# Masking the scores of a sparse graph-attention layer in PSUM with a signed bound, in place of multiplying the exponentials by mask bytes

## The chip, the cores and the metric

The kernel runs on one core of one Trainium2 chip, in one launch. The metric is the device time of that launch in microseconds (us). The kernel before was timed three times: 2150.40, 2150.49 and 2156.22 us, median 2150.49. A profile was taken of one execution of it.

A core has five engines, each with its own instruction queue that it works off in order: PE (TensorE, matrix products), DVE (VectorE, elementwise work and reductions), ACT (ScalarE, functions of one input with a scale and a bias), POOL (GpSimd, here mostly the engine that issues gathers) and SP (SyncE, here a queue for DMAs). SBUF is the on-chip working memory of 128 partitions. PSUM holds the results of products[...].

## What is computed

Two graph layers over 4096 nodes with 512 features each. The adjacency `adj` is 4096 x 4096 float32, symmetric in where it is nonzero, with a full diagonal; an off-diagonal entry is nonzero with a chance of a bit under 0.8%. The change is in the second layer:

```python
# layer 0
h = relu(layernorm(x));  x = x + relu(normalized(adj) @ h @ W0 + b0)
# layer 1
h = relu(layernorm(x))
Wh = h @ W;  e = leaky_relu(Wh @ a[:F] + (Wh @ a[F:]).T, 0.2)
mask = adj > 0
attention = softmax(where(mask, e, -1e12), axis=1)
negative_attention = -softmax(where(mask, -e, -1e12), axis=1)
out = elu(concat([attention @ h, negative_attention @ h], axis=1) @ wtrans)
x = x + out
```

So for each node i layer 1 needs, over the neighbours j of i, the weights exp(e) and exp(-e) with e = leaky_relu(s_i + t_j), their sums, and the sums of h_j with these weights.

## The kernel before

**Layer 0** is dense. It reads `adj` and its transpose, normalizes, and multiplies. On the way it also prepares layer 1: it writes one row per node into a table in HBM (eight copies, one for each eighth of the nodes i). A row has 644 words: the 512 features of h, the score t in word 512 (`ROW_T`), and from word 516 (`ROW_W`) on 512 mask bytes, one for each node of that eighth, which are 1 where the two nodes are neighbours and 0 elsewhere. It also lists, for each pair of 64-node blocks, the rows that these blocks need.

**Layer 1** (`sparse_layer1`, L1316) works by blocks of 64 nodes i (`RB`). There are 64 blocks, two to a pair. The first pair (`PAIR0`) is worked within layer 0 by code of its own (L1203 to L1313); the other 31 pairs, 62 blocks, are the loop that the change touches. Per pair:

- `gather1` (L1340) issues 22 indirect DMAs from POOL through `gather` (L469, the issue itself is L473): each fetches 128 table rows into SBUF. The 22 chunks go into three tiles, a = 0, 1, 2, with 8, 6 and 8 chunks. The even block of the pair uses tiles 0 and 1, the odd block tiles 1 and 2. Six tile slots exist, so two pairs are held at a time, and a gather has to wait until the block that used its slot two pairs earlier has been worked through.
- `weights(r)` (L1351) makes the weights of a block r, in two parts, one for each of its two tiles: 8 chunks x 64 nodes (128 x 512 elements) and 6 chunks (128 x 384). For each part, `scores` (L486, DVE at L487) adds t and s into a PSUM bank `z`; ACT makes `y` = 0.2 z (L1361); DVE takes the larger of the two into z (L1362); `exps` (L491, ACT at L499) writes exp(z) and exp(-z) into the SBUF tile `p` for g = 0 and 1; `mask_out` (L503, DVE at L509) multiplies each of the two by (mask byte > 0), in place in `p`, the mask bytes being read from the gathered rows. After both parts DVE sums the whole of `p` over its chunks into `total` (L1367).
- `product(r)` (L1370) multiplies the weights with the gathered rows on PE, 44 instructions (L516), makes the inverse sums (L540 on PE, L542 and L543 on DVE), and ACT writes the scaled result `us` (L1383).
- `turn(r)` (L1385) transposes `us` on PE (`tp`, L550), and ACT copies it to `ut` (L555).
- `finish1(j)` (L1390), once per pair, multiplies by `wtrans` with 16 instructions on PE (L1397), takes elu and adds x (L1405 to L1409), and stores.

**The order.** The loop from L1438 on lists, for step k: `product` of block k, the gathers of the pair two ahead (tile 0 at an even step, tiles 1 and 2 at an odd one), `weights` of block k + 2, `turn` of block k - 1, and at odd steps `finish1`. That is the program's order. Where nothing is pinned with `keep_in_program_order`, a planner may place instructions of one engine in another order, as far as their data allow. In the trace it has done so: on DVE the scores of a block's second part often stand ahead of the mask products of its first part, and on ACT `us` of an even block k stands behind the exponentials of both parts of block k + 2. The gathers are pinned, and so are the exponentials of the first four blocks.

Of the kernel before, what the change touches and what calls it, by code (L numbers as in the profile page):

```python
# [8 lines left out]
F32 = mybir.dt.float32  # L9
U8 = mybir.dt.uint8  # L10
# [3 lines left out]
AF = mybir.ActivationFunctionType  # L14
ALU = mybir.AluOpType
# [4 lines left out]
P = 128  # L20
# [10 lines left out]
RB = 64  # L31
# [16 lines left out]
ROW_W = 516  # L48
ROW = 644
MAXS = 40.0  # L50
TINY = 2.0**-110


# [214 lines left out]
def gcn_gat_kernel(  # L268
# [26 lines left out]
    nc = tc.nc  # L295
# [15 lines left out]
    RPT = NR // NTAB  # L311
# [12 lines left out]
    def bank(name):  # L324
        return ps.tile([P, 512], F32, tag="ps", name=name)
# [4 lines left out]
    with sbuf(name="init", bufs=1) as init:  # L330
        column = init.tile([P, P], F32, name="column")
        nc.vector.memset(column[:, 0:1], 0.0)
        n = 1
# [150 lines left out]
    def scores(s, z, t):  # L484

        n = z.shape[1]  # L486
        return nc.vector.tensor_tensor(  # L487
            z, t.to_broadcast([P, n, RB]), s.unsqueeze(1).to_broadcast([P, n, RB]), ALU.add
        )

    def exps(z, p, bound=False, pin=False, leaky=True):  # L491

        if leaky:
            nc.vector.scalar_tensor_tensor(z, z, ALPHA, z, ALU.mult, ALU.max)
        if bound:
            nc.vector.tensor_scalar(z, z, 2 * MAXS, -2 * MAXS, ALU.min, ALU.max)
        z = z.rearrange("p k (h i) -> p k h i", h=2)
        for g in range(2):
            i = nc.scalar.activation(p[:, :, :, g], z, AF.Exp, scale=(1.0, -1.0)[g])  # L499
            if pin:  # L500
                tc.keep_in_program_order(i)

    def mask_out(r, p, mask):  # L503

        m = mask[:, :, r % RPT * RB : (r % RPT + 1) * RB]
        m = m.rearrange("p k (h i) -> p k h i", h=2)
        for g in range(2):
            e = p[:, :, :, g]
            nc.vector.scalar_tensor_tensor(e, m, 0.0, e, ALU.is_gt, ALU.mult)  # L509
# [50 lines left out]
    with sbuf(name="y0", bufs=1) as y_pool, sbuf(name="wa", bufs=1) as wa_pool, sbuf(name="bits", bufs=4) as bits_pool, sbuf(name="small0", bufs=4) as small, ExitStack() as rest, ExitStack() as lists:  # L560
# [224 lines left out]
        def scale(yp, j):  # L785

            rs = small.tile([P, 2], F32, tag="rs", name=f"rs{j}")
            nc.vector.tensor_reduce(rs[:, 0:1], parts.pop(j), AX.X, ALU.add)
            nc.vector.tensor_scalar(rs[:, 1:2], rs[:, 0:1], TINY, None, ALU.max)
            nc.vector.reciprocal(rs[:, 1:2], rs[:, 1:2])  # L790
# [209 lines left out]
        i0, n = GROUPS[0]  # L1000
# [89 lines left out]
        def judge(small):  # L1090
# [11 lines left out]
            for g, vec in enumerate((s_all, t_all)):  # L1102
# [3 lines left out]
                nc.vector.tensor_scalar(  # L1106
                    ok[:, 2 + g : 3 + g], ok[:, 2 + g : 3 + g], MAXS * MAXS, None, ALU.is_le
                )
# [94 lines left out]
        with sbuf(name="work2", bufs=2) as work, sbuf(name="sums2", bufs=2) as sum_pool, sbuf(name="at2", bufs=4) as at_pool, sbuf(name="scratch", bufs=1) as scratch, sbuf(name="pair", bufs=1) as pair:  # L1203
# [95 lines left out]
            k = late0 % EJ  # L1299
# [16 lines left out]
    def sparse_layer1():  # L1316
        nonlocal verdict
        with ExitStack() as pools:

            def pool(name, bufs):  # L1320
                return pools.enter_context(sbuf(name=name, bufs=bufs))
# [3 lines left out]
            g_pools = {s: pool("g%d%d" % s, 1) for s in slots}  # L1325
            tmp, small, p_pool = pool("tmp", 1), pool("small1", 2), pool("p", 3)
            work, ut_pool, s_pool, wt_pool = pool("work1", 2), pool("ut", 2), pool("s", 2), pool("wt", 1)
            warm = small.tile([P, 1], F32, tag="warm", name="warm", bufs=1)
            nc.scalar.activation(warm, sign, AF.Exp)
            wt_sb = wt_pool.tile([P, 2 * FC, F], F32, name="wt_sb")  # L1330
# [15 lines left out]
            def parts(r):  # L1346

                t = gath[r // 2][r % 2 : r % 2 + 2]
                return (t[0], 0, t[0].shape[1]), (t[1], t[0].shape[1], t[1].shape[1])

            def weights(r):  # L1351

                nk = sum(CHUNKS[r % 2 : r % 2 + 2])
                p = p_pool.tile([P, nk, 2, 2, SB], F32, tag="p", name=f"p{r}")
                s = srow[r // 8][:, r % 8 * RB : (r % 8 + 1) * RB]

                for gt, k, n in parts(r):
                    z = bank(f"z{r}_{k}")[:, : n * RB].rearrange("p (k c) -> p k c", c=RB)
                    scores(s, z, gt[:, :, ROW_T : ROW_T + 1].bitcast(F32))
                    y = tmp.tile([P, n, RB], F32, tag=f"y{n}", name=f"y{r}_{k}")  # L1360
                    nc.scalar.activation(y, z, AF.Copy, scale=ALPHA)  # L1361
                    nc.vector.tensor_tensor(z, z, y, ALU.max)  # L1362
                    exps(z, p[:, k : k + n], leaky=False, pin=r in first)
                    mask_out(r, p[:, k : k + n], gt[:, :, ROW_W:].bitcast(U8))
                total = small.tile([P, 2 * RB], F32, tag="total", name=f"total{r}", bufs=3)
                q = p.rearrange("p k h g i -> p (h g i) k")
                nc.vector.tensor_reduce(total, q, AX.X, ALU.add)  # L1367
                wgt[r] = (p, total)
# [46 lines left out]
            first = order[:4]  # L1415
# [14 lines left out]
            for a in range(3):  # L1430
                gather1(pairs[1], a)
            weights(order[0])
            weights(order[1])

            tc.keep_in_program_order(
                nc.scalar.dma_start(out=wt_sb, in_=wtrans.rearrange("(c p) f -> p c f", p=P))
            )
            for k, r in enumerate(order):  # L1438
                product(r)
                if k % 6 == 1 and k // 6 < len(later):  # L1440
                    for j, n in GROUPS[-2:]:
                        queue = nc.scalar if k == 1 else nc.sync
                        tc.keep_in_program_order(copy_rows(queue, later[k // 6], j, n))
                if k + 4 - k % 2 < len(order):
                    for a in ((0,), (1, 2))[k % 2]:
                        gather1(order[k + 4 - k % 2] // 2, a)
                if k + 2 < len(order):
                    weights(order[k + 2])
                    if wanted and order[k + 2] % 8 == 7:
                        load_s(wanted.pop(0))  # L1450
                if k:
                    turn(order[k - 1])
                if k == 2:
                    finish1(PAIR0)
                if k == 40:
                    verdict = judge(small)
                if k % 2 and k > 1:
                    finish1(order[k - 3] // 2)
            turn(order[-1])
            finish1(order[-1] // 2)  # L1460

    sparse_layer1()
    bad = nc.values_load(
        verdict[0:1, 0:1],
# [38 lines left out]
```

## Time and profile before

| | us |
|---|---|
| three timed runs: lowest, median, highest | 2150.40, 2150.49, 2156.22 |
| the profiled execution: span from its first to its last instruction | 2033.7 |
| the median less that span | 116.8 |
| first gather of the 31 pairs; the last one ends | 1086.2; 1981.8 |
| PE's last instruction ends | about 2024 |

For the profiled execution the span is the only time on record; what lies around it is read here from the median of the timed runs. Times in the profile are counted from the span's start. A row of a view by groups names line, engine, operation and tiles (output first), the shapes, how many there were (x...), their busy time, the mean in ns, and then the idle time of the engine just before them and who ended it. In a timeline a row gives start, length, engine, line and operation, and in brackets the idle time before it. The granted clock of PE is 0.976 of full on average over the span.

### The profile page before, as it was taken

How to read it: one execution, taken by the hardware profiler on the slowest of the kernel's cores; microseconds unless marked ns; L12 is line 12 of the kernel's file. 1: busy time of each engine (PE TensorE's matmuls, PEld its weight loads, DVE VectorE, ACT ScalarE, POOL GpSimd, SP SyncE). 2: the span in 40 equal slices, each digit the busy share in tenths (PEclk: the TensorE clock that was granted, in tenths of full speed). 3: DMA queues.
4: the chain of work that ended last, by engine and by line, in shares of the span. 5: the costliest groups of instructions: out<-in, count | busy, mean ns of one | idle time of the engine just before them, and what ended most of it. 6: DMA issues, size and time to landing. Idle time of an engine off the chain costs nothing.

```text
span 2033.7 us, 23721 instructions
## 1 busy us (share of the span) xinstructions
PE 1884.8 (93%) x7832; PEld 1066.1 (52%) x7832; DVE 1279.9 (63%) x2907; ACT 626.0 (31%) x1181; POOL 932.4 (46%) x1047
## 2 busy tenths in 40 slices
PE   6999999897999999979996799999999999999998
PEld 3433337786788888868771233333333333333333
DVE  6555558989793538983354566566665656566653
ACT  5766652212112221212032233233322332333321
POOL 3000001133331113233064777777777777777770
PEclk9999999998999999989997899999999999999999
DMA  9988869467448565728384989989898898888880
GB/s 364 328 298 283 298 201 325 135 217 244 137 142 280 187 232 173 250 87 287 93 258 142 324 291 307 290 288 307 275 308 282 292 310 274 279 265 271 278 274 30
DMA packets 181115, 503.53 MB, mean 248 GB/s; under 512 B 27091, under 2 KB 35699, under 8 KB 180982
## 3 DMA queue, kind: packets, MB, share of 16 engines
q0 software_dynamic: 73184, 275.36, 42.1%
q1 hardware_dynamic: 77808, 171.80, 25.6%
q10 hardware_dynamic: 29990, 54.75, 7.7%
q8 instruction: 64, 1.05, 0.2%
q14 instruction: 69, 0.57, 0.1%
HBM read 409.89 MB, written 103.02 MB: 252 GB/s over the span
## 4 chain that ended last, share of the span: by engine, by line
POOL 16%; PE 13%; DMA 9%; issue 7%; DVE 4%; ACT 1%; DVEq 0%; POOLq 0%
POOL g L473 16%; DMA g<-table,idx 9%; PE u L516 7%; PE o L1397 5%; DVE p L509 1%; DVE z L487 1%; PE tp L550 1%; ACT p L499 1%; DVE z L1362 1%; ACT us L1383 0%; DMA table<-h 0%; DVE prod L895 0%; DVE stb L455 0%; DVE total L1367 0%; ACT y L1361 0%
## 5 line engine op out<-in xcount | busy, mean ns | idle before, releaser
L473 POOL DMA_INDIRECT g<-table,idx x704 | 701.4, 996 | 230.0 <-issue 209.3
L516 PE MATMUL u<-g,p 128*64 128x512 f32 x2816 | 628.6, 602 | 18.0 <-DVE p L509 13.2
L516 PEld LDWEIGHTS u<-g,p 128*64 128x64 f32 x2816 | 199.4, 139 | 394.1 <-issue 354.4
L972 PE MATMUL p<-t,sums 128*128 128x256 f32 x896 | 268.5, 384 | 15.2 <-DVE sums L960 10.4
L972 PE MATMUL p<-y,at 128*128 128x256 f32 x896 | 272.0, 386 | 3.6 <-DVE w L855 2.5
L487 DVE TENSOR_TENSOR z<-g,s 128x512 f32<-128x512 f32 (+1 forms) x124 | 78.4, 634 | 311.2 <-DMA g<-table,idx 298.1
L972 PE MATMUL p<-y,sums 128*128 128x256 f32 x896 | 270.6, 384 | 0.8 <-DVE sums L962 0.8
L1361 ACT ACTIVATE y<-z 128x512 f32<-128x512 f32 (+1 forms) x124 | 67.5, 544 | 553.1 <-DVE z L487 427.0
L1397 PE MATMUL o<-wt_sb,ut 128*128 128x512 f32 x512 | 228.3, 599 | 0.5 <-ACT ut L555 0.5
L432 POOL DMA_INDIRECT ld<-li,off x112 | 102.8, 918 | 258.7 <-DMA ld<-li,off 199.2
L812 ACT ACTIVATE m<-at 128x1024 uint8<-128x1024 f32 x110 | 115.0, 1053 | 339.7 <-DMA at<-in_adj_t 289.5
L1367 DVE TENSOR_REDUCE total<-p 128x128 f32<-128x1792 f32 x62 | 201.5, 3250 | 2.1
L972 PEld LDWEIGHTS p<-t,sums 128*128 128x128 f32 x896 | 171.8, 193 | 41.9 <-DVE sums L960 12.8
L972 PEld LDWEIGHTS p<-y,at 128*128 128x128 f32 x896 | 171.3, 193 | 32.1 <-DVE w L855 3.7
L972 PEld LDWEIGHTS p<-y,sums 128*128 128x128 f32 x896 | 173.1, 193 | 25.6 <-DVE sums L962 1.2
L509 DVE SCALAR_TENSOR_TENSOR p<-g,p 128x384 f32<-128x384 uint8 (+1 forms) x256 | 145.5, 619 | 23.3 <-ACT p L499 23.3
L821 POOL DMA_DIRECT2D table<-m x71 | 56.4, 795 | 220.3 <-ACT m L812 136.2
L747 ACT ACTIVATE junk<-ar 128x1024 bf16<-128x1024 f32 x128 | 134.7, 1052 | 72.1 <-DMA ar<-in_adj 70.8
L1397 PEld LDWEIGHTS o<-wt_sb,ut 128*128 128x128 f32 x512 | 96.0, 193 | 109.8 <-issue 108.9
L972 PE MATMUL p<-t,at 128*128 128x256 f32 x448 | 136.8, 388 | 9.6 <-DVE w L855 7.6
L499 ACT ACTIVATE p<-z 128x512 f32<-128x512 f32 (+2 forms) x252 | 123.6, 549 | 65.2 <-DVE z L1362 56.5
L776 PE MATMUL yp<-w_sb,hx_t 128*128 128x512 f32 x256 | 120.1, 613 | 2.9 <-DVE hx_t L729 2.9
(198 smaller groups left out, 1811.7 us busy)
## 6 DMA issues: line engine op xcount, KB each, us to landing
ar<-in_adj SPq DMA_DIRECT2D x128, 512.0 KB, 7.5
at<-in_adj_t SPq DMA_DIRECT2D x112, 512.0 KB, 4.1
table<-h ACTq DMA_DIRECT2D x182, 258.0 KB, 5.9
table<-m POOLq DMA_DIRECT2D x55, 256.0 KB, 4.9
g<-table,idx POOLq DMA_INDIRECT x704, 4.5
at<-in_adj_t SPq DMA_DIRECT2D x32, 256.0 KB, 7.8
xr<-in_x SPq DMA_DIRECT2D x32, 256.0 KB, 6.5
x1d<-y POOLq DMA_DIRECT2D x32, 256.0 KB, 5.3
```

The source lines that it names most:

```text
L432: return nc.gpsimd.indirect_dma_start(out=lst_dram[g][:, :], out_offset=bass.IndirectOffsetOnAxis(ap=off[g][:, e, c : c + 1], axis=0), in_ ...
L473: i = nc.gpsimd.indirect_dma_start(out=gt[:, k, :], out_offset=None, in_=table[2 * n // RPT], in_offset=bass.IndirectOffsetOnAxis(ap=idx[n ...
L487: return nc.vector.tensor_tensor(z, t.to_broadcast([P, n, RB]), s.unsqueeze(1).to_broadcast([P, n, RB]), ALU.add)
L499: i = nc.scalar.activation(p[:, :, :, g], z, AF.Exp, scale=(1.0, -1.0)[g])
L509: nc.vector.scalar_tensor_tensor(e, m, 0.0, e, ALU.is_gt, ALU.mult)
L516: i = nc.tensor.matmul(u[h * RB : (h + 1) * RB], p[:, k, h].rearrange("p g i -> p (g i)"), row(k), start=k == HALVES[r % 2][h][0], stop=en ...
L747: nc.scalar.activation(junk, ar, AF.Identity, accum_out=part[:, c : c + 1]),
L776: nc.tensor.matmul(yp, hx_t[j][:, c * P : (c + 1) * P], w0_sb[:, c, :], start=c == 0, stop=c == FC - 1,)
L812: nc.scalar.activation(m, at, AF.Sign)
L972: i = nc.tensor.matmul(out, left[:, x * P : (x + 1) * P], right, start=jp == 0 and first, stop=jp == NP - 1 and (final or not first),)
L1367: nc.vector.tensor_reduce(total, q, AX.X, ALU.add)
L1397: nc.tensor.matmul(po, ut[:, g, c, :], wt_sb[:, g * FC + c, :], start=g == 0 and c == 0, stop=g == 1 and c == FC - 1,)
```

## The change

`weights` no longer calls `exps` and `mask_out`. ACT makes from the mask bytes a float32 tile `m` that holds +1000 where the byte is 1 and -1000 where it is 0. DVE makes y = max(-m, z), which is z at a neighbour and 1000 elsewhere, and z = min(z, m), which is z at a neighbour and -1000 elsewhere. The exponentials are then taken of z and of -y, so that both vanish elsewhere. The pair worked within layer 0 keeps `exps` and `mask_out`.

```diff
@@ constants
+FAR = 1000.0
@@ sparse_layer1
+            far = small.tile([P, 1], F32, tag="far", name="far", bufs=1)
+            nc.gpsimd.memset(far, -FAR)
@@ weights(r), for each of the two parts
                     scores(s, z, gt[:, :, ROW_T : ROW_T + 1].bitcast(F32))
+                    m = tmp.tile([P, n, RB], F32, tag=f"m{n}", name=f"m{r}_{k}")
+                    bits = gt[:, :, ROW_W:].bitcast(U8)
+                    nc.scalar.activation(
+                        m,
+                        bits[:, :, r % RPT * RB : (r % RPT + 1) * RB],
+                        AF.Identity,
+                        scale=2 * FAR,
+                        bias=far,
+                    )
                     y = tmp.tile([P, n, RB], F32, tag=f"y{n}", name=f"y{r}_{k}")
                     nc.scalar.activation(y, z, AF.Copy, scale=ALPHA)
                     nc.vector.tensor_tensor(z, z, y, ALU.max)
-                    exps(z, p[:, k : k + n], leaky=False, pin=r in first)
-                    mask_out(r, p[:, k : k + n], gt[:, :, ROW_W:].bitcast(U8))
+                    nc.vector.scalar_tensor_tensor(y, m, -1.0, z, ALU.mult, ALU.max)
+                    nc.vector.tensor_tensor(z, z, m, ALU.min)
+                    for g, x in enumerate((z, y)):
+                        i = nc.scalar.activation(
+                            p[:, k : k + n, :, g],
+                            x.rearrange("p k (h i) -> p k h i", h=2),
+                            AF.Exp,
+                            scale=(1.0, -1.0)[g],
+                        )
+                        if r in first:
+                            tc.keep_in_program_order(i)
```

## The prediction

> **What bounds the kernel now.** The change touches only the loop over the 31 pairs, so I read that stage alone, first by slices of 40 us (columns: length, busy us and instructions of each engine, PE clock, DMA share, GB/s).
>
> ```profile
> 1560.00:1600.00 40.00, 37.22 (x156) 13.95 (x153) 22.79 (x33) 11.03 (x23) 30.57 (x32) 0.96 0.92 311
> 1840.00:1880.00 40.00, 38.80 (x160) 15.10 (x160) 26.26 (x37) 12.83 (x28) 30.56 (x32) 1.00 0.87 268
> 1960.00:2000.00 40.00, 38.48 (x172) 14.62 (x170) 24.44 (x36) 11.96 (x27) 16.84 (x17) 1.00 0.56 183
> ```
>
> PE is busy 93 to 97%, DVE 60%, ACT 30%. POOL shows only 76%, but the same 31 or 32 gathers in every slice until they are all issued. The waits of this stage (1160 to 2034) say what that means:
>
> ```profile
> POOL g L473 <- issue: 179.0, 588, 0.3
> ...
> PE tp L550 <- ACT us L1383: 27.4, 21, 2.9
> ```
>
> POOL's idle time is 0.3 us ahead of each gather, never more: no slot, no semaphore holds it up, it is working flat out. PE loses 27.4 us, all at one place: the transpose of an even block waits for `us`, which stands in ACT's queue behind exponentials that wait for gathered rows. The chain of waits from 1100 on agrees:
>
> ```profile
> by line: POOL g L473 32.2%; DMA g<-table,idx 18.2%; issue 14.0%; PE u L516 13.4%; PE o L1397 11.4%; DVE p L509 2.3%; DVE z L487 1.6%; PE tp L550 1.4%; DVE z L1362 1.3%; ACT p L499 1.2%; ACT us L1383 0.7%; DVE total L1367 0.3%; ACT y L1361 0
> ```
>
> Now the two paces. PE without a wait needs 27.46 us per pair (in its timeline the products with `wtrans` start at 1610.31 and 1637.77 with no idle entry between). POOL starts a gather every 1302.6 ns on average (622 intervals from 1170 to 1982): 22 x 1.3026 = 28.66 us per pair. So POOL sets the pace and PE waits about 1.2 us per pair; 28 pairs of that are the 27 us above. But most gathers are faster. POOL's and DVE's timelines of the same stretch:
>
> ```profile
> 1516.41 0.95 POOL L473 DMA_INDIRECT g<-table,idx  x1 [0.30 <-issue]
> 1517.66 1.33 POOL L473 DMA_INDIRECT g<-table,idx  x1 [0.31 <-DMA g<-table,idx]
> 1519.29 0.95 POOL L473 DMA_INDIRECT g<-table,idx  x1 [0.30 <-DVE z L1362]
> 1520.54 1.11 POOL L473 DMA_INDIRECT g<-table,idx  x1 [0.30 <-issue]
> 1521.96 0.94 POOL L473 DMA_INDIRECT g<-table,idx  x1 [0.30 <-issue]
> ```
>
> ```profile
> 1517.48 1.29 DVE L509 SCALAR_TENSOR_TENSOR p<-g,p 128x512 f32<-128x512 uint8 x2
> 1518.69 0.56 DVE L1362 TENSOR_TENSOR z<-z,y 128x384 f32<-128x384 f32 x1
> 1519.80 1.03 DVE L509 SCALAR_TENSOR_TENSOR p<-g,p 128x384 f32<-128x384 uint8 x2 [0.56 <-ACT p L499]
> 1520.87 3.25 DVE L1367 TENSOR_REDUCE total<-p 128x128 f32<-128x1792 f32 x1
> ```
>
> The gathers at 1517.66 and 1520.54 start inside a mask product (L509) and last 1.33 and 1.11 us; those beside L1362 and the reduction keep 0.95. I set every gather of the stage beside the DVE instruction that runs at its start. Of 84 that start within L509, 79 are stretched; within the scores (L487), 18 of 47; within L1362 0 of 62, within L1367 0 of 151, beside an idle DVE 0 of 230. The stretch is what is left of the DVE instruction less 0.125 us. Over the layer all stretches sum to 34.8 us, 28.0 of them by L509 and about 6 by L487.
>
> [...]L509 reads mask bytes and `p`, both in SBUF, L487 reads t and s, both in SBUF; L1362 has one input in PSUM. [...]
>
> **The change part by part.**
>
> ```profile
> L509 DVE SCALAR_TENSOR_TENSOR p<-g,p 128x512 f32<-128x512 uint8 x118 | 75.9, 684 | 1.8 <-ACT p L499 1.8
> L509 DVE SCALAR_TENSOR_TENSOR p<-g,p 128x384 f32<-128x384 uint8 x116 | 59.5, 554 | 15.7 <-ACT p L499 15.7
> ...
> L1362 DVE TENSOR_TENSOR z<-z,y 128x512 f32<-128x512 f32 x58 | 40.0, 689 | 3.5
> L1362 DVE TENSOR_TENSOR z<-z,y 128x384 f32<-128x384 f32 x58 | 32.4, 558 | 0.0
> ...
> L1408 DVE SCALAR_TENSOR_TENSOR y<-o,x 128x512 f32<-128x512 f32 x32 | 21.8, 681 | 0.0
> ```
>
> *DVE's count and time do not change.* There are 124 parts. Two mask products each (684 or 554 ns) go; a max (as L1408, 681 ns) and a min (as L1362, 689 or 558 ns) come. 248 x 0.62 = 154 us go, as much comes, on an engine that is 60% busy: 0.
>
> *What changes is where DVE reads.* Both new instructions take `m` from SBUF and z from PSUM: one SBUF input. By L1362 (62 starts within it, none stretched) they should not hold up POOL. Their output may matter: the max writes SBUF as L1408 does, which only one gather met well inside (at 1182.6, 0.52 us left), unstretched. Bound of the stretches that go: 28.0 us if neither new form contends, about 14 if one does, 0 if both. I take 28.0.
>
> *ACT gets 124 activations.* [...] Behind it in ACT's queue stand y, the exponentials, `us` and the `ut` copies. It needs only the gathered rows, as the scores do that y waits for already[...]: about +0.1 us. The byte form is not in the stage's trace; 0.5 (as L1361) to 1.0 us changes that by 0.4 at most.
>
> *The way from rows to `us` gets longer.* Before: scores at 1517.01, `us` at 1520.04, 3.03 us. The last mask products did not lie on it, only the exponentials. Now max and min stand ahead of the exponentials: 2 x 0.5 us more in the queue, less the part of L509's 1.29 us that stood between (0.5): with ACT's 0.1, +0.7 us; up to +2 if the planner lets the first part's max and min wait behind the second part's scores. It is a shift, paid once, not per pair, as long as POOL never waits for PE. A slot of tile 0 came free at 1511.8 and was filled from 1523.2 on, so 11.4 us of lag is room.
>
> *The reduction* now waits for the last exponential in place of a DVE product (about 1 us); the scores behind it on DVE wait mostly for rows anyway (276.7 us in all), and the total is needed a block later: 0. The memset of `far` is one POOL instruction (0.13 us, as L1094). Reading y from SBUF in the second exponential costs ACT at most 0.04 us each: 0. Buffers of `m`, single, are freed by the min, well before the next part of that size.
>
> **The sum.** I replay the pairs: PE reaches the transpose of pair n at the later of its previous one + 27.46 us, and the time at which `us` was ready before, less the L509 stretches up to there, plus 0.7. At the last gated transpose (1980.97) PE is then 25.5 us ahead; what follows (52.7 us) is PE's own work and stays. POOL's new pace is 22 x 1.248 + 0.2 = 27.65 us, so the two engines are nearly even, and PE, no longer POOL alone, ends the gain: the 28.0 us can't all be had. Cross-check: PE idles 27.6 us in this stage, and two stretches at a lowered clock, after waits of 2.7 us, cost 1.6 us each: 30.8 at most. L487's stretches can grow, as its place against the gathers moves; scores that wait for rows start 0.6 us after a gather and end before the next one, so I allow 1 us in all. Gain 24.5 us: span 2009.2. Outside the span lie 116.8 us by the median; they stay: 2126.0 us. The profiled execution has no time of its own beside its span, so this stands on the median of three, two of which agree within 0.1 us.
>
> **The rivals.** (1) *DMA takes POOL's place.* For: the DMA share is 0.92 while the table's late rows are copied, and landings then take up to 9 us against 4.5. Against: it falls back within a pair, and 0.87 x 1.035 is 0.90. If nothing is gained until about 1570, half the pairs remain: 2138. (2) *`us` gets behind a later tile.* The new activation needs only rows; if the planner puts that of the next block ahead of `us`, PE waits for tile 2, which lands about 8.6 us after tile 1: a shift, 2135. (3) *Slower: the loop closes.* The same, with the next block's exponentials in front too: 8.6 us + some 4.8 of work = 13.4, above the 11.4 us of room. Gathers then wait for slots: 2 us of excess per two pairs, 28 pairs, 28 us, plus the shift of 13.4: 2167. It decides at a lag of 11.4 us; against it speaks that ACT is idle 60% and that `us` is ready first. (4) *The contention stays*, since it is the operation and not the place of its inputs: the gain is nothing, and +0.7 gives 2151. Against: L1408 is the same operation. (5) *Better*: `us` is placed further forward, and no wait is left: 2119.
>
> **How the numbers follow.** A measurement here can tell about 0.3% (6.5 us) from no change. Forecast 0.62 (2120 to 2132), (1) 0.09, (2) 0.12, (3) 0.05, (4) 0.07, (5) 0.05. Faster are forecast, (1), (2) and (5): 0.88; same (4): 0.07; slower (3): 0.05. Leaving out (3) and (4) leaves 0.88, so the range runs from a little under (5), 2116, to a little over (1), 2143; a changed start of the stage (PE waits for the first rows there, up to 6.7 us at a time) is within it.
>
> **What would show it.** Gathers at 0.95 us throughout but for those that meet L487; about 1.255 us from gather to gather; PE's wait for `us` below 8 us; no stretched gather within the two new DVE lines; `us` some 3.7 us after its scores. It would be wrong if POOL has waits over 0.3 us, if landings pass 6 us for many pairs in a row, or if gathers still stretch within the new max or min.

## The result and the profile after

The kernel after took 2182.99 us (four runs, 2171.47 to 2191.27), the kernel before beside it 2151.24 (four runs, 2150.4 to 2156.22): a ratio of 1.013, 95% interval 1.009 to 1.017. It is slower, where 2126 was forecast with a range of 2116 to 2143.

The kernel before took 2027 to 2033 us (medians) in some groups of runs (called A here) and 2151 to 2163 us in others (called B), the runs beside the result are of B, and the trace of before that the forecast was read from, which spans 2033.7 us, was of A; so I compare only within a group. In the runs that list both, time less span is 1.8 us (2.2 in e12): the 116.8 us that I had put outside the span were the difference between A and B.

The slices of the kernel after that answer to those of before (length, busy us and instructions of PE, PE's loads, DVE, ACT and POOL, PE clock, DMA share, GB/s):

```profile
1560.00:1600.00 40.00, 33.70 (x120) 12.64 (x118) 22.07 (x35) 14.87 (x30) 23.26 (x25) 0.91 0.72 225
1840.00:1880.00 40.00, 36.10 (x133) 13.05 (x131) 18.82 (x28) 12.67 (x26) 25.07 (x27) 0.96 0.82 259
1960.00:2000.00 40.00, 34.03 (x121) 12.07 (x120) 17.55 (x25) 12.94 (x26) 25.22 (x27) 0.91 0.75 225
```

POOL issues 25 to 27 gathers in 40 us where it issued 31 or 32, and PE is busy less, at a lower clock. No engine is busy without a break. The waits from 1160 on (engine and line, what it waited for: us in all, times, longest):

```profile
POOL g L474 <- issue: 246.8, 576, 6.9
...
DVE total L1388 <- ACT p L1378: 125.0, 42, 8.6
...
PE u L517 <- issue: 64.8, 79, 2.2
...
POOL g L474 <- ACT p L1378: 48.1, 13, 8.8
```

The longest wait of a gather was 0.3 us in before; it is 8.8 us now. All but one stand ahead of the first gather of a tile, when its slot has to come free, and they sum to 149 us beyond the usual 0.3. PE's wait for `us`, 27.4 us in before, has no entry of its own any more; in its place PE stops inside its products. Who ended a wait is told from semaphore records, and the names are not safe here: the trace holds 944 updates of one DMA semaphore that has 2003 in a trace of before. The chain of waits from 1100 on, with the same caution:

```profile
by line: PE u L517 64.1%; PE o L1418 20.7%; issue 9.1%; PE tp L551 3.5%; PE cs L541 0.8%; DMA g<-table,idx 0.4%; POOL g L474 0.3%; ACT p L1378 0.1%; DVE eo L1426 0.1%; DVE eo L1430 0.1%; ACT eo L1427 0.1%; ACT m L1365 0.1%; ACT y L1373 0.0%
```

POOL had 32% of it and has 0.3%; PE's products have 64%. What they look like, in PE's timeline of the kernel after, and a product of before under it:

```profile
1636.77 3.65 PE L517 MATMUL u<-g,p 128*64 128x512 f32 x15
1641.48 0.59 PE L517 MATMUL u<-g,p 128*64 128x512 f32 x1 [1.07 <-issue]
1642.90 0.85 PE L517 MATMUL u<-g,p 128*64 128x512 f32 x1 [0.83 <-issue]
1644.28 1.01 PE L517 MATMUL u<-g,p 128*64 128x512 f32 x1 [0.54 <-issue]
1645.68 1.86 PE L517 MATMUL u<-g,p 128*64 128x512 f32 x2 [0.39 <-issue]
...
```

```profile
1600.22 9.66 PE L516 MATMUL u<-g,p 128*64 128x512 f32 x44
```

44 records in 9.66 us is the even pace. In the kernel after single records start 1.4 us apart for a while, and the 44 records of this product take 18.1 us. From the third of the 31 pairs on, a product of an even block lasts 12.3 us on average and one of an odd block 11.8: 4.8 us more per pair than at the even pace. The gathers' pace is 33.2 us per pair here.

The part of the forecast that was about the stretched gathers can be read in the same trace, POOL first and DVE under it:

```profile
1522.57 0.95 POOL L474 DMA_INDIRECT g<-table,idx  x1 [0.30 <-issue]
...
1530.37 0.94 POOL L474 DMA_INDIRECT g<-table,idx  x1 [3.10 <-ACT p L1378]
...
1535.36 1.39 POOL L474 DMA_INDIRECT g<-table,idx  x1 [0.30 <-issue]
```

```profile
1522.34 0.56 DVE L1376 TENSOR_TENSOR z<-z,m 128x384 f32<-128x384 f32 x1
...
1530.10 0.68 DVE L1375 SCALAR_TENSOR_TENSOR y<-m,z 128x512 f32<-128x512 f32 x1
...
1535.26 0.68 DVE L488 TENSOR_TENSOR z<-g,s 128x512 f32<-128x512 f32 x1
```

A gather that starts inside the new min (L1376) or the new max (L1375) lasts 0.95 us, one that starts inside the scores (L488) is stretched to 1.39. (The 3.10 us ahead of the second gather are a wait for a slot.) And the sizes, by shape (busy us, mean ns of one):

```profile
L1365 ACT ACTIVATE m<-g,far 128x512 f32<-128x512 uint8 x61 | 43.9, 720 | 173.9 <-DMA g<-table,idx 127.6 <-issue 46.1
...
L1376 DVE TENSOR_TENSOR z<-z,m 128x512 f32<-128x512 f32 x62 | 42.9, 693 | 0.0
L1375 DVE SCALAR_TENSOR_TENSOR y<-m,z 128x512 f32<-128x512 f32 x62 | 42.1, 680 | 0.2
...
L1365 ACT ACTIVATE m<-g,far 128x384 f32<-128x384 uint8 x62 | 37.8, 610 | 111.3 <-DMA g<-table,idx 98.5 <-issue 12.6
```

m costs 720 and 610 ns; no activation of this form stands in the stage that the forecast was read from, so its length there was my estimate. max costs 680 ns where L1408 cost 681, min 693 where L1362 cost 689. What the forecast did not have is the last column of L1365: ACT stands still for 174 and 111 us ahead of m, mostly for gathered rows; in a trace of A (e7, below), whose semaphore records are complete, it is 174 and 151 us.

### The profile page after: what moved, and what is told of

The parts are those of the page before. It is cut to its first block, busy times and chain, and to the rows that moved or that the text cites. A ratio compares the mean times of both kernels' runs of the same rounds, so it can differ in the third digit from the quotient of the medians.

```text
span 2169.7 us, 24236 instructions
## 1 busy us (share of the span) xinstructions
PE 1976.2 (91%) x7832; PEld 1093.3 (50%) x7832; DVE 1281.5 (59%) x2907; ACT 710.6 (33%) x1305; POOL 916.0 (42%) x1048
## 4 chain that ended last, share of the span: by engine, by line
PE 45%; issue 5%; DVE 1%; POOL 1%; DMA 1%; ACT 0%; ACTq 0%; POOLq 0%; DVEq 0%
PE u L517 32%; PE o L1418 10%; PE tp L551 2%; POOL g L474 1%; PE cs L541 0%; DMA g<-table,idx 0%; DMA table<-h 0%; DVE prod L896 0%; DVE stb L456 0%; DMA table<-m 0%; DVE y L835 0%; DVE y L888 0%; DVE p L510 0%; POOL table L822 0%; ACT L500 0%
## 5 line engine op out<-in xcount | busy, mean ns | idle before, releaser
L474 POOL DMA_INDIRECT g<-table,idx x704 | 683.8, 971 | 379.6 <-issue 278.0
L517 PE MATMUL u<-g,p 128*64 128x512 f32 x2816 | 719.7, 622 | 101.7 <-issue 89.7
L517 PEld LDWEIGHTS u<-g,p 128*64 128x64 f32 x2816 | 226.5, 142 | 541.8 <-issue 518.0
L1365 ACT ACTIVATE m<-g,far 128x512 f32<-128x512 uint8 (+1 forms) x124 | 82.3, 665 | 285.1 <-DMA g<-table,idx 226.1
L1426 DVE TENSOR_SCALAR eo<-o 128x512 f32<-128x512 f32 x32 | 22.1, 692 | 220.6 <-remote 71.0
L932 PE MATMUL acc<-y,at 128*128 128x512 f32 x256 | 121.9, 601 | 0.0
L1378 ACT ACTIVATE p<-y 128x512 f32<-128x512 f32 (+1 forms) x124 | 71.1, 574 | 96.4 <-DVE y L1375 49.5
```

Source lines behind the costliest of these rows:

```text
L474: i = nc.gpsimd.indirect_dma_start(out=gt[:, k, :], out_offset=None, in_=table[2 * n // RPT], in_offset=bass.IndirectOffsetOnAxis(ap=idx[n ...
L517: i = nc.tensor.matmul(u[h * RB : (h + 1) * RB], p[:, k, h].rearrange("p g i -> p (g i)"), row(k), start=k == HALVES[r % 2][h][0], stop=en ...
L932: nc.tensor.matmul(a, at[:, 0, it * P : (it + 1) * P], y0[j], start=j == 0, stop=j == NJ - 1)
L1365: nc.scalar.activation(m, bits[:, :, r % RPT * RB : (r % RPT + 1) * RB], AF.Identity, scale=2 * FAR, bias=far,)
L1378: i = nc.scalar.activation(p[:, k : k + n, :, g], x.rearrange("p k (h i) -> p k h i", h=2), AF.Exp, scale=(1.0, -1.0)[g],)
```

## The experiments

The theories. Q: the planner put m too far forward in ACT's queue, where an m that waits for the rows of a later tile holds back exponentials and `us` that were ready. T: m's work itself, or ACT as a third reader of the rows, costs wherever it stands. B: y is held until its exponential, so that single buffers make DVE and ACT wait. Two more came later. C: the queue's order costs little unless the conditions of B make gathers wait. P: in group B it is PE and the slots that set the pace, so stretches that go are worth nothing there.

Four numbers of each trace are used, over the pairs from the third on: us per pair from gather to gather; the sum of all that gathers last beyond 0.96 us (stretches); the tail, from the last gather's end to the end of DVE's last instruction; and the time from the landing of the second tile's last rows to the last write of the even block's `p` from it (rows to p, the median over the pairs).

| kernel, group A | us per pair | stretches, us | tail, us | rows to p, us |
|---|---|---|---|---|
| before (e1) | 28.56 | 29.1 | 44.3 | 4.8 |
| after (e7) | 28.18 | 18.8 | 51.8 | 12.9 |
| m behind y (e2) | 27.88 | 10.1 | 44.0 | 4.1 |
| no m (e3) | 27.88 | 10.3 | 44.4 | 4.1 |
| before with m added (e4) | 28.54 | 28.4 | 50.3 | 13.1 |
| only the third tile's m held (e12) | 28.07 | 13.9 | 47.4 | 7.5 |
| all but the third's held (e13) | 27.76 | 7.0 | 50.9 | 12.5 |

**Before again (e1, e6, e10, e14).** No edit.

> The kernel before, unchanged, for a second trace of it. The first trace has a span of 2033.7 us, 117 us under the timed runs, which my forecast put down to time around the span; the trace of the kernel after has only 1.8 us around it. If it was time around the span, this trace again spans about 2034 us beside a time of 2150. If the first trace was of an execution that ran faster than the timed ones, this one spans 2148 to 2150 us, and the layer-1 loop or an earlier stage is longer in it; then the pace of 28.66 us per pair, from which I reckoned, may be wrong too.

> The kernel before once more, to have its trace from the same chip as the three kernels beside it. The runs so far fall into two groups: one chip where before takes 2028 us and PE's products run evenly, and conditions (the result's runs and the repeat of after) where before takes 2151 to 2154 and the trace of after shows stretches of 7 to 16 us in which PE starts a pair of products every 704 ns in place of 423 ns[...]. If such stretches are a property of the chip, the trace of before has them too where its time is 2151 (about 120 us of them) and has none where its time is 2028.

> The kernel before, for a trace beside the next three. Where its time is 2025 to 2040: gathers never wait, 28.6 us per pair, as in three traces so far. Where its time is 2151: if the cause is that PE is slowed down there (starts of product pairs 704 ns apart in place of 423), the gathers of before wait for slots too, 100 to 130 us in all, and its stretches cost nothing; if not, the gathers run at 28.6 us per pair and the 120 us lie elsewhere.

> The kernel before, for a trace where it takes 2151, if the conditions are those. Theory P (PE slowed there, so that it sets the pace): gathers wait for slots 100 to 130 us in all and PE starts pairs 704 ns apart in stretches. Otherwise 28.6 us per pair with no wait, as in four traces.

Measured: 2026.94, 2040.87, 2031.86 and 2028.62 us, with spans 1.8 us less, in groups where before's runs had a median of 2027.8, 2032.7, 2027.3 and 2029.5. The pace is 28.6 us per pair and no gather waits, as in the trace that I forecast from. So the reading of before was right for A, and no trace of before without extra work was had in B.

**After again (e5, e7).** No edit.

> The kernel after, unchanged, because the kernel before took 2027.8 us in the last experiments, where its timed runs beside the result had taken 2151, so the result was taken under conditions that the experiments did not share. Theory Q (m in ScalarE's queue ahead of exponentials and `us` makes the gathers wait for slots): slower than before here too, 2040 to 2065 beside 2028. Theory C (the conditions of the result's runs closed the loop through the slots for both kernels, and with rows landing in time the queue's order costs little; the kernel before with m added took 2035 with no gather waiting): 2008 to 2025, faster than before, gathers waiting nowhere.

> The kernel after beside before and the two next kernels. Where before takes 2151: 2170 to 2190 as measured twice. Where before takes 2028: theory Q (ScalarE's queue alone closes the loop through the slots) says slower than before, 2040 to 2065; theory C (the queue's order costs only where PE is slowed down as well, since the kernel before with m added took 2035 with no gather waiting) says 2012 to 2025, faster than before by 0.2 to 0.8%, gathers waiting nowhere.

Measured: e5 fell into B, 2177.49 us beside 2153.53, ratio 1.011 (1.007 to 1.015), with 147 us of gathers waiting for slots: the result repeated. e7 fell into A, 2030.81 beside 2032.71, ratio 0.999 (0.998 to 1.000). In A the change is worth almost nothing, and no gather waits: neither Q's 2040 nor C's 2012 to 2025 is met. The gain in stretches is 10 us in place of 28, and 7.5 us are lost again in the tail.

**m behind y (e2, e8, e11, e15).** The activation that makes m is held behind y of its own part (shortened: `bits` stands for the slice of mask bytes).

```diff
-nc.scalar.activation(m, bits, AF.Identity, scale=2 * FAR, bias=far)
-nc.scalar.activation(y, z, AF.Copy, scale=ALPHA)
+i = nc.scalar.activation(y, z, AF.Copy, scale=ALPHA)
+with tc.issue_after(i.ins):
+    nc.scalar.activation(m, bits, AF.Identity, scale=2 * FAR, bias=far)
```

> The kernel after, with each bound m held behind the ScalarE copy y of its own part, so that no m stands ahead of exponentials of an earlier part or ahead of `us`. Theory Q (ScalarE's queue: an m that waits for the rows of a later tile holds up exponentials and `us` behind it, PE gets p late and the gathers wait for slots): 2126 us, 2116 to 2140, gathers never wait over 0.5 us. Theory T (ScalarE's extra 82 us and the third reader of the rows cost it, in whatever order): 2170 to 2190 as after. Theory B (y is now held until its exponential, m and y have one buffer each, so VectorE and ScalarE wait for each other): 2165 to 2185.

> The kernel after with m held behind y of its own part, beside the others. Where before takes 2028: 2010 again. Where before takes 2151: theory Q says the order is what costs, so 2125 to 2140, faster than before; theory T (ScalarE's extra work and third reader) says 2165 to 2185, as after.

> The kernel after with every m held behind y of its own part. Where before takes 2025 to 2040: 1.0% less, as twice. Where before takes 2151: theory P (there PE sets the pace through the slots, so stretches that go are worth nothing, and what costs is PE's later start behind the queue) says 2145 to 2155, no change; theory Q says 2125 to 2140.

> The kernel after with every m behind y of its own part. Where before takes 2151: 2145 to 2155 by theory P, 2125 to 2140 by theory Q. Elsewhere 0.8 to 1.1% under before, as three times.

Measured, all in A: 2010.6, 2014.79, 2010.83 and 2012.71 us; ratios to before 0.991 (0.988 to 0.994), 0.990 (0.988 to 0.992), 0.992 (0.990 to 0.995) and 0.993 (0.990 to 0.995). Same instructions, another place in one queue, and the change is worth 16 to 18 us. ACT's timeline in the kernel after (e7), and with m behind y (e8) under it:

```profile
1517.04 0.48 ACT L1373 ACTIVATE y<-z 128x384 f32<-128x384 f32 x1
1524.09 0.72 ACT L1365 ACTIVATE m<-g,far 128x512 f32<-128x512 uint8 x1 [6.56 <-DMA g<-table,idx]
1524.71 0.51 ACT L1378 ACTIVATE p<-y 128x384 f32<-128x384 f32 x1
1525.13 0.47 ACT L1378 ACTIVATE p<-z 128x384 f32<-128x384 f32 x1
```

```profile
1516.98 0.49 ACT L1366 ACTIVATE y<-z 128x384 f32<-128x384 f32 x1 [2.94 <-DVE z L488]
1517.37 0.60 ACT L1368 ACTIVATE m<-g,far 128x384 f32<-128x384 uint8 x1
1518.76 0.52 ACT L1379 ACTIVATE p<-y 128x384 f32<-128x384 f32 x1 [0.79 <-DVE y L1376]
1519.24 0.49 ACT L1379 ACTIVATE p<-z 128x384 f32<-128x384 f32 x1
```

In the kernel after the exponentials of the second tile's part (128x384) start 7.2 us after the end of its y, because an m of 128x512, the third tile's, stands between and waits 6.56 us for rows. With m behind y they start 1.3 us after it. The gathers wait for nothing in either:

```profile
POOL g L474 <- issue: 175.3, 576, 0.3
```

```profile
POOL g L474 <- issue: 177.6, 583, 0.3
```

**No m (e3, e9).** The activation is left out; max and min read two tiles filled once with +1000, so nothing is masked out (shortened; the lines that make the two tiles are not shown).

```diff
-m = tmp.tile([P, n, RB], F32, tag=f"m{n}", name=f"m{r}_{k}")
-nc.scalar.activation(m, bits, AF.Identity, scale=2 * FAR, bias=far)
+m = bound[n]
```

> The kernel after without the 124 activations that make m: the max and the min read two constant tiles filled with the bound once, so nothing is masked out (the adjacency inside the gathered rows is ignored), while VectorE's instructions, y's use and the exponentials stay. Theory Q: 2115 to 2130 us, what the missing stretches of gathers are worth. Theory T: the same. Theory B: 2160 to 2185, as y is still held until its exponential.

> The kernel after without the activations that make m (two constant tiles in their place, so nothing is masked out), beside the others. Where before takes 2028: 2006 again. Where before takes 2151: theories Q and T both say 2120 to 2140; theory B (y held until its exponential, PE's weights come later) says 2160 to 2180.

Measured, in A: 2006.54 and 2013.3 us, ratios 0.989 (0.987 to 0.991) and 0.990 (0.988 to 0.992), the same as with m behind y. Theory B falls, for y is held here too. Theory T falls for A: 82 us of activations cost at most a few us when they stand in the right place (2010.6 against 2006.5, 2014.8 against 2013.3).

**Before with m added (e4).** The activation at its place, its result unused; L509 stays (shortened, against the kernel before).

```diff
+nc.scalar.activation(m, bits, AF.Identity, scale=2 * FAR, bias=far)
 nc.scalar.activation(y, z, AF.Copy, scale=ALPHA)
 ...
 mask_out(r, p[:, k : k + n], gt[:, :, ROW_W:].bitcast(U8))
```

> The kernel before with the activation that makes m added at its place, its result unused; the mask products stay. Theory Q: the stretches stay and the queue's waits come, so slower than before and not faster than after: 2180 to 2215 us, with POOL waiting some us per pair. Theory T: 2160 to 2190. Theory B: 2150 to 2155, as nothing of y changes.

Measured, in A: 2035.11 beside 2027.82, ratio 1.004 (1.002 to 1.006). Slower, but by 7 us and with no gather waiting, so not as Q had it: rows to p go from 4.8 to 13.1 us, and what is paid is the tail, 6 us, once.

**Which m (e12, e13).** `issue_after` only for the third tile's m, or only for the others (the one line that differs; where `late` is false, m stays ahead of y).

```diff
+late = r % 2 == 1 and k > 0    # e13: not (...)
```

> The kernel after with only the m of the odd block's second part (third tile, the pair's last rows) held behind y; the m of the first and second tile stay early. Theory Q3 (the one that costs is this m, as it holds back the exponentials of the even block's second part until the pair's last rows have landed, 10 us): 1.0% under before, tail after the last gather 44 to 46 us, stretches 9 to 12 us. Theory Q1 (the m of the next pair's first tile, ahead of `us`, costs as much): 0.3 to 0.6% under before, tail 48 to 51 us. Where before takes 2151: within 0.5% of before by Q3, 1% over it by Q1.

> The reverse: the m of the first and second tile held behind y, the one of the third tile early. Theory Q3: as the kernel after, within 0.2% of before, tail 50 to 53 us, stretches 16 to 20 us. Theory Q1: 0.4 to 0.8% under before. Where before takes 2151: 1.0 to 1.4% over before by Q3, 0.3 to 0.8% by Q1.

Measured, in A: e12 2018.36, ratio 0.995 (0.993 to 0.997); e13 2016.74, ratio 0.994 (0.991 to 0.996). Each recovers about half of what all of them do. The times are those of Q1 in both, those of Q3 in neither: no single m costs it all. The third tile's m alone, left early (e13), brings the late p and a tail of 50.9 us, but few stretches. The early m of the other tiles (e12) bring 3 us of tail and 4 us of stretches inside the output sum (L1430 in the kernel after, L1409 in before), which has two SBUF inputs and stretched no gather in before.

**PE loaded (e16, e17, e18).** Each block does its first five pairs of products once more than needed, in the kernels before, after, and with m behind y.

```diff
+half_products(r, u, p, row, [c[:5] for c in HALVES[r % 2]])
 half_products(r, u, p, row, HALVES[r % 2])
```

> The kernel before with PE slowed on purpose: each of the 62 blocks first does its first 5 pairs of products once more than needed (their sums are started anew afterwards), 5 x 0.423 = 2.1 us a block, 4.2 us a pair, so PE needs 27.46 + 4.23 = 31.7 us per pair and is behind POOL's 28.6. Expected 2028 + 30 x 3.1 = 2120, 2105 to 2140 by every theory; gathers wait for slots about 3 us a pair, like those of the kernel after where before took 2151.

> The kernel after with the same extra products. Theory P (where PE sets the pace, stretches that go are worth nothing, while ScalarE's order still makes PE start later): 5 to 30 us above the kernel before with the extra products, as the result shows it (26 to 32 us). Theory R (the loss where before takes 2151 comes from something else of those conditions, not from PE's being the bound): within 5 us of it, or faster.

> The kernel with every m behind y of its own part, with the same extra products. Theory P: within 4 us of the kernel before with the extra products, since the stretches are hidden behind PE and the queue's order is as before. If it is 15 us under it, the stretches count even where PE sets the pace; if it lies with the kernel after, m's work on ScalarE costs and not its place.

These fell into B, where before took 2163.08: 2292.89, 2324.36 and 2320.04 us, ratios to before 1.060 (1.057 to 1.062), 1.074 (1.070 to 1.077) and 1.073 (1.071 to 1.076). I had halved the load: one product shows as two records (22 products of a block in the program, 44 in the trace), and 0.423 us is the time of two records, so the five pairs are ten times 0.423 us a block. A product in which PE nowhere stops takes 13.95 us with it and 9.66 without, so PE gets 8.6 us more per pair, 36.0 with its own 27.46. The trace of e16 has 36.4 us per pair. POOL's waits in e16, and a slice:

```profile
POOL g L473 <- PE u L516: 215.7, 54, 10.5
POOL g L473 <- issue: 167.9, 539, 3.9
```

```profile
1560.00:1600.00 40.00, 40.00 (x178) 15.98 (x174) 18.24 (x27) 8.87 (x19) 25.43 (x26) 1.00 0.77 239
```

PE is busy throughout, and POOL waits for PE to free slots: what gathers lose by being stretched (45 us in e16, 7 in e18) is then on no path. The kernel after is 31 us above e16, with m behind y 27: the gain is gone, as P says, but the order is not what costs here, as P had it; my 4 us for e18 were wrong. By what was expected of e18, this points to m's work and not its place; but the new DVE instructions came with it, and no loaded run without m tells the two apart. From the third pair's product on, the loss sits in one place. A product of an odd block lasts 13.95 us in all three traces; one of an even block 14.07 in e16, 14.77 in e17 and 15.13 in e18 on average. Over 29 pairs these 0.70 and 1.06 us are 20 and 31 us, and that is all by which the three differ from there to the last product's end. (The third pair's product itself starts 16 us later in e17 than in e16 and 8 us earlier in e18, which is not explained.) A typical one of e18 in PE's timeline:

```profile
1404.62 7.46 PE L517 MATMUL u<-g,p 128*64 128x512 f32 x33
...
1412.89 3.66 PE L517 MATMUL u<-g,p 128*64 128x512 f32 x16 [0.82 <-issue]
```

PE stops in the middle of the even block's product: here one record starts 1.41 us after the one before it. It isn't a late p or late rows: nearly all products at this place repeat ones of the extra load, which had read the same rows and the same `p` a few us before. In 26 of the 29 even products of e18 from the third pair on, and in 23 of those of e17, late starts (0.5 to 0.7 us apart mostly in e17, 0.7 or 1.4 us mostly in e18) end 8.6 to 9.1 us after the product's start, whichever record PE has reached by then; in e16 a single product has one, at 8.25 us. So they look like the slow starts in the kernel after. What sets them off, the trace doesn't say.

## Why the prediction was wrong, point by point

*What bounds the kernel* ("POOL's idle time is 0.3 us ahead of each gather, never more"): true of A, four more traces agree (28.55 to 28.61 us per pair). One sum in it is off: 28 pairs at 1.2 us would be 33.6 us, not the 27.4 that PE waits; the forecast went by the waits, so nothing hangs on it. The timed runs that the forecast had to meet were of B. There the gathers of the kernel after wait 147 to 149 us for slots, those of before with PE loaded 210 us, so POOL does not set the pace alone. **This is the first step that failed**: "Outside the span lie 116.8 us by the median; they stay". It is 1.8 us. A span 117 us below the timed runs was a sign that the trace and the times were of different conditions, and I took it for time around the span.

*The sum.* Beside the traced execution's own span of 2033.7 the same sum said 2009.2, and e2, which has the order that the sum assumed, spans 2010.0. That nearness is luck: before took 2027.8 in e2's group, so its gain is 17 us and not 24.5. In A the kernel after gains 1.9 us; 16 more come when m stands behind y (e7 against e8), the other 7 of the 24.5 go with the stretches that stayed (9 of the 28 us, below). In B it loses 32. If A's share may be carried over, some 23 of the 57 us between 2126 and 2183 are the terms below, and the other 34 are what B adds.

*The stretches that go* (28.0 us by L509): right in direction, too large in size. Over the last 29 pairs of a trace L509 made 22.8 to 25.9 us of them, and no gather is stretched by the new forms. With more than 0.2 us of the DVE instruction left, e7 has 33 starts inside L1375 and 28 inside L1376, none stretched, against 72 of 77 inside L509 in e1. Both have one input in SBUF and one in PSUM, as L1362, within which none of 62 starts was stretched in before; that L1375 writes SBUF made no difference. That it is a second SBUF input which makes a DVE instruction stretch gathers stays my reading of these lines; no run moves an input alone. Mis-sized was "L487's stretches can grow, so I allow 1 us": the scores (L488) make 8.4 to 10.0 us in e2, e3 and e8 and 14.6 in e7, where before had 3.7 to 6.4, and the output sum (L1430) 4.2 in e7 from 0. Net, 10 us of stretches go in the kernel after, 19 with m behind y. The pace with m behind y is 27.88 against a forecast of 27.65.

*DVE's count and time* (0): right, 1281.5 us busy after, 1279.9 before.

*ACT gets 124 activations* (hidden, "It needs only the gathered rows, as the scores do that y waits for already", "about +0.1 us"): the length was my estimate, with no activation of this form in the stage to show it. Measured, the 124 take 82.3 us, 720 and 610 ns each (in before `us` at L1383, of 128x512 too, took 692), and ACT is busy 40 and 42% of the slices at 1560 and 1840 in e7, where before had 28 and 32%. The exponential that reads y from SBUF takes 33 and 35 ns more there than the one that reads z from PSUM (630 and 515 against 597 and 480), within the 0.04 us allowed. What was wrong is the place. **This is the second step that failed.** m doesn't wait beside its own y; the planner has placed it ahead of work of earlier blocks, and there it waits for rows (174 and 151 us in e7) while ready work stands behind it. Rows to p is not +0.1 but +8.1 us (4.8 to 12.9), in e13 with the third tile's m alone +7.7. That m, which needs only rows, moves forward is the mechanism of my rival (2), where I named `us` as the one behind it and 8.6 us as the shift; exponentials and `us` are both behind it.

*The way from rows to `us`* (+0.7 us, a shift paid once): from the scores of the even block's second tile to `us` it is 3.03 us in before, 3.25 with m behind y and 8.5 in e7 (medians), so +0.2 with the order that was assumed and +5.4 with the planner's. In A it is paid once, as tail: 7.5 us in e7. In B gathers do wait for slots, so the condition for this is not met; what a lag costs there, no run shows.

*The reduction* (0): it now waits 125 us for exponentials in the kernel after and 190 in e7. PE's product that needs it (`cs`) has 0.8% of the chain, so no cost is seen; none was measured apart.

*The rivals.* The measured 2183 lies nearest rival (3), slower through slots, and its sign that would show it ("POOL has waits over 0.3 us") is there. Its mechanism is not confirmed: in A the lag passed 8 us and no gather waited; in B gathers waited whatever the order (e18). So for B this much is shown: with PE loaded POOL waits for PE, stretches don't count, and the kernel after loses some 0.7 to 1.1 us per pair inside the even block's product, with m held or not. The cause of the 32 us by which the kernel after is slower in B stays open: no trace of before without the load was had there, and no run there tells whether m behind y, or no m at all, is above or below before.

## What to carry to other kernels

Before pricing an instruction as "hidden", find its place in its engine's queue: a planner may place an instruction with few inputs early, as it did with m, and if that waits on data of a later tile, everything ready behind it waits too (here 7.2 us in place of 1.3); hold it behind an instruction that needs the same data. Check that the traced span and the timed runs are of the same conditions before adding the difference to a forecast; here a gap of 117 us was not time around the span. And what a contention costs an engine counted here only where that engine never waited: with m behind y the edit gave 1% where gathers ran freely, and no gain with PE loaded, where they waited for slots.

## What was not expected of the hardware

The same kernel takes longer in B than in A, before by 6% and after by 7%, with the same transfers: the median packet of the gathers takes 198 ns in both, and a gather's last packet comes 3.2 to 3.6 us after the gather's end on average in both. What differs is PE: in the two traces of the kernel after in B its product records start 704, 1410 or 2100 ns apart for 5 to 30 us at a time, where they start in pairs every 423 ns in A. Between the third pair and the last gather the granted clock is at 0.5 for 82 to 107 us in these two, for 3 to 20 us in the traces of A. In the trace beside the result the pieces at 0.5 last 3.41, 6.83 or 10.24 us. From 1260 us to the last gather 138 product records start there 0.6 us or more after the one before, 67 of them at a granted clock of 1.00; ten of these lie between 1713 and 1727 us, with no piece at 0.5 within 50 us. So the granted clock alone does not explain the slow starts. In e16, where PE is busy throughout, such starts and the pieces at 0.5 are gone from about 1235 us until the last gather. Each trace of B holds 20,300 to 20,900 semaphore records, each of A 30,200 to 30,350, so the releasers named in B can't be relied on. It is not simply the chip: the record gives the number 10 to a chip with runs of A (e10 to e13) and to one with runs of B (e16 to e18). What sets B apart was not found.
